# Four product tiles instead of three, the softmax subtraction and the statistics placed earlier, and one block of convolution products placed a slice later

## The chip, the cores and the metric

One core of one Trainium2 chip. The metric is device time in microseconds of the whole program, median of the runs; lower is better.

## The reference

The input is 16 images of 56 x 56 pixels with 384 channels, float32. Two layers, each added to its input:

```python
x = x + attention(group_norm(x), w_qkv, w_proj, b_proj)
x = x + depthwise_3x3(group_norm(x), sign(clip(w)))
```

- `group_norm`: 32 groups of 12 channels, over all pixels of an image.
- `attention`: a 1x1 projection to q, k, v. The 384 channels form three groups of 128, with dilations 1, 2, 3. In each group of four heads of 32 channels, every pixel attends to its 3 x 3 neighbours at that dilation: nine scores per head, softmax, weighted sum of v. Then a 1x1 output projection with bias.
- `depthwise_3x3`: each channel convolved with its own 3 x 3 kernel of signs, zero padding.

## The kernel before

**Tiling.** Channels lie on partitions, in three blocks of 128. An image is cut into 7 chunks of 8 rows, 448 pixels. Each chunk goes through three plans: `plan_a` (load, transpose, channel statistics of the input), `plan_b` (the attention layer, residual and statistics of its result, written to DRAM as `x1d`), `plan_c` (the convolution layer and the output). The 112 chunks are pipelined: while `plan_b` works on chunk m, `plan_a` is some chunks ahead and `plan_c` ten chunks behind.

**Order of the work.** Time is counted in slices, nine to a chunk (`STEP`). Each plan registers small pieces with `at(slice, order, piece)`; at the end the pieces are emitted sorted by slice, and inside a slice by the constants `SOFTMAX, SCORE, STATISTICS, CONVOLVE, WEIGH, ... PROJECT, ... LOADS`. A scheduler then takes this emitted program and decides on each engine's own instruction order, from its estimate of when each instruction is ready, with the emitted order as priority. Each engine runs its list in order. Tiles come from pools with a fixed number of buffers; a new tile takes the buffer that came free longest ago, and its writer waits until the last reader of that buffer is done.

**Attention of one chunk (`plan_b`).**
- `score(i)`, nine times: VectorE (DVE) writes `t` = q times three shifted k (L517), TensorE (PE) adds them over the head's channels into `ps` (L502).
- `softmax_1` to `softmax_5`: ScalarE (ACT) copies `ps` to `sT` (L534), PE transposes, DVE takes maximum and difference (L540, L541), ACT the exponential (L542), DVE the sum, reciprocal and product `ew` (L546 to L548). ACT casts `ew` to bf16 into `e3` (`e<-ew`, L556). GpSimd (POOL) computes `rest` = `ew` minus that cast (L560, `softmax_4`) and writes two further bf16 terms of it (L564, L565, `softmax_5`). The sum of the three terms stands for the float32 weight.
- `turn_weights`: a transposing DMA from SP's queue turns `e3` into `aT` (L570). It cannot start before L565 is done.
- `weigh(i)`, nine times, three for each group: PE spreads the weights over channels into the single PSUM tile `pb_a` (L583, three matmuls), DVE multiplies by v into a tile `w` (L590), and POOL adds the second and the third `w` of a group to the first (L598), then the three thirds to `y` (L601, L602). `w` has three buffers.
- `out_project`: PE (L616), DVE adds bias and residual into `xr` (L619) and takes statistics (L622).

**Convolution of one chunk (`plan_c`).** Channels 0 to 255 go through PE: `load` brings three shifted copies of `x1d` into `z` (L684), ACT normalises them (`z<-z`, L697, four instructions per block), POOL zeroes the padding before and after (L678, L699), PE convolves (L711), DVE adds (L718). Channels 256 to 383 go through ACT and POOL: ACT normalises into `zg` (L740), `taps_g(ky)` writes three products (`m<-zg`, L762), POOL adds the blocks (L768) and the thirds (L773, L776). In the first chunk of an image (`c == 0`) the whole group is one slice later (`late = 1`), since the statistics of that image are only just there. `turn(s)` transposes back through `osb` (L788), sent out from SP's queue (L791).

**Statistics.** `statistics(when, sets)` runs `group_norm` in six steps; the first aggregates per-channel statistics with six instructions (L310) at one slice. From the third image on, each call serves the second layer of image b and the first layer of image b + 2 at once.

**Last image.** `plan_c` of image 15 borrows tiles of the attention, `w` among them (`z_last`, L675).

Of the kernel before, what the change touches and what calls it, by code (L numbers as in the profile page):

```python
# [8 lines left out]
F32 = mybir.dt.float32  # L9
# [8 lines left out]
P = 128  # L18
HEADS = 4
HD = 32  # L20
NG = 3
# [3 lines left out]
SUB = 112  # L25
# [3 lines left out]
NPAD = 32  # L29
# [6 lines left out]
def dilated_attention_then_binary_conv(  # L36
# [28 lines left out]
    nc = tc.nc  # L65
    B, H, W, C = x.shape
    PX = ROWS * W
    NCH = H // ROWS
    NSUB = PX // SUB
# [12 lines left out]
    of = out.rearrange("b h w c -> b (h w) c")  # L82
# [65 lines left out]
    xn_p = ctx.enter_context(tc.tile_pool(name="xn_p", bufs=3))  # L148
    xr_p = ctx.enter_context(tc.tile_pool(name="xr_p", bufs=1))
    t_p = ctx.enter_context(tc.tile_pool(name="t_p", bufs=4))  # L150
    w_p = ctx.enter_context(tc.tile_pool(name="w_p", bufs=3))
    y_p = ctx.enter_context(tc.tile_pool(name="y_p", bufs=4))
    s_p = ctx.enter_context(tc.tile_pool(name="s_p", bufs=1))
    a_p = ctx.enter_context(tc.tile_pool(name="a_p", bufs=2))
    x1_p = ctx.enter_context(tc.tile_pool(name="x1_p", bufs=2))
    xg_p = ctx.enter_context(tc.tile_pool(name="xg_p", bufs=2))
    m_p = ctx.enter_context(tc.tile_pool(name="m_p", bufs=3))
    o_p = ctx.enter_context(tc.tile_pool(name="o_p", bufs=3))


    kv = []
# [134 lines left out]
    def group_norm(sets):  # L296

        had = {}
        L = len(sets)

        def channels():
            had["ch"] = ch = st_p.tile([P, L, NG, 2], F32, tag=f"ch{L}", name="ch")
            for n, (stats, _, _) in enumerate(sets):
                for j in range(NG):
                    nc.vector.bn_aggr(ch[:, n, j, :], stats[:, j].rearrange("p c s -> p (c s)"))  # L310

        def mean():
            had["pair"] = pair = st_p.tile([GN_G, L, 3], F32, tag=f"pair{L}", name="pair")
            pm = ps_mt.tile([P, 512], F32, tag="mt", name="pm")
            for j in range(NG):
                nc.tensor.matmul(
                    pm[:GN_G, 0:L], gsel[:, j], had["ch"][:, :, j, 0], start=(j == 0), stop=(j == NG - 1)
                )
            nc.vector.tensor_scalar_mul(pair[:, :, 2], pm[:GN_G, 0:L], -1.0 / GN_CH)

        def deviation():

            ch = had["ch"]
            pb = ps_mt.tile([P, 512], F32, tag="mt", name="pb")
            for j in range(NG):
                nc.tensor.matmul(
                    pb[:, j * L : (j + 1) * L], gselT[:, j], had["pair"][:, :, 2], start=True, stop=True
                )
            had["dev"] = dev = st_p.tile([P, L, NG], F32, tag=f"dev{L}", name="dev")
            nc.vector.tensor_tensor(  # L330
                dev, pb[:, : NG * L].rearrange("p (j l) -> p l j", l=L), ch[:, :, :, 0], ALU.add
            )
            nc.gpsimd.tensor_tensor(dev, dev, dev, ALU.mult)
            nc.gpsimd.tensor_tensor(dev, dev, ch[:, :, :, 1], ALU.add)

        def variance():
            dev = had["dev"]
            pv = ps_mt.tile([P, 512], F32, tag="mt", name="pv")
            for j in range(NG):
                nc.tensor.matmul(pv[:GN_G, 0:L], gsel[:, j], dev[:, :, j], start=(j == 0), stop=(j == NG - 1))  # L340
            had["var"] = var = st_p.tile([GN_G, 3, L], F32, tag=f"var{L}", name="var")
            v, r = var[:, 0], var[:, 1]
            nc.vector.tensor_scalar(v, pv[:GN_G, 0:L], 1.0 / GN_CH, 1e-5, op0=ALU.mult, op1=ALU.add)

            ri = r.bitcast(I32)
            nc.vector.tensor_single_scalar(ri, v.bitcast(I32), 1, op=ALU.arith_shift_right)
            nc.vector.tensor_scalar(ri, ri, -1, RSQRT_BITS, op0=ALU.mult, op1=ALU.add)

        def invert():

            var, pair = had["var"], had["pair"]
            v, r, t = var[:, 0], var[:, 1], var[:, 2]
            for step in range(3):
                nc.gpsimd.tensor_tensor(t, r, r, ALU.mult)
                nc.gpsimd.tensor_tensor(t, t, v, ALU.mult)
                nc.gpsimd.tensor_scalar(t, t, -0.5, 1.5, op0=ALU.mult, op1=ALU.add)
                nc.gpsimd.tensor_tensor(pair[:, :, 1] if step == 2 else r, r, t, ALU.mult)
            nc.gpsimd.tensor_tensor(pair[:, :, 0], pair[:, :, 2], pair[:, :, 1], ALU.mult)

        def spread_out():  # L360
            pair = had["pair"]
            pp = ps_mt.tile([P, 512], F32, tag="mt", name="pp")
            for j in range(NG):
                nc.tensor.matmul(
                    pp[:, 2 * L * j : 2 * L * (j + 1)], gselT[:, j], pair[:, :, 0:2], start=True, stop=True
                )
            mr = st_p.tile([P, NG, L, 2], F32, tag=f"mr{L}", name="mr", bufs=5 - L)
            nc.vector.tensor_copy(mr.rearrange("p j l s -> p (j l s)"), pp[:, : 2 * L * NG])
            for n, (_, done, for_convolution) in enumerate(sets):
                if not for_convolution:  # L370
                    done(mr[:, :, n])
                    continue

                pz = ps_mt.tile([P, 512], F32, tag="mt", name="pz")
                for s in range(JG * NQ):
                    of_set = gselT[:, s // NQ, s % NQ * HD : s % NQ * HD + HD]
                    for ky in range(3):
                        nc.tensor.matmul(
                            pz[ky * HD : (ky + 1) * HD, 2 * s : 2 * s + 2], of_set, pair[:, n, 0:2],
                            start=True, stop=True,  # L380
                        )
                mrz = st_p.tile([K3, JG, NQ, 2], F32, tag="mrz", name="mrz")
                nc.vector.tensor_copy(mrz.rearrange("p j q s -> p (j q s)"), pz[:K3, : 2 * JG * NQ])
                done(mr[:, :, n], mrz)

        return channels, mean, deviation, variance, invert, spread_out
# [6 lines left out]
    def at(when, order, piece):  # L393

        pieces.setdefault((when, order), []).append(piece)
# [50 lines left out]
    def plan_b(m, t0):  # L446
# [83 lines left out]

        def softmax_1():

            sT = s_p.tile([P, PX], F32, tag="sT", name="sT")
            nc.scalar.copy(sT, had.pop("ps")[:, :PX])  # L534
            pt = ps_mt.tile([P, 512], F32, tag="mt", name="pt_s")
            for s in range(NSUB):
                nc.tensor.transpose(pt[:SUB, s * P : (s + 1) * P], sT[:, s * SUB : (s + 1) * SUB], permf)
            pt4 = pt[:SUB].rearrange("p (s v) -> p s v", s=NSUB)[:, :, :NR]
            mx = s_p.tile([SUB, NSUB, GH], F32, tag="mx", name="mx")
            nc.vector.reduce_max(mx, by_neighbour(pt4).rearrange("p s o k -> p s k o"), axis=AX.X)  # L540
            nc.vector.tensor_tensor(by_neighbour(weights), by_neighbour(pt4), over_neighbours(mx), ALU.subtract)  # L541
            nc.scalar.activation(weights, weights, AF.Exp, scale=SCALE)  # L542
# [13 lines left out]
            nc.scalar.copy(term[0], e8)  # L556

        def softmax_4():
            had["rest"] = rest = s_p.tile([SUB, NSUB * NPAD * HEADS], F32, tag="rest", name="rest")
            nc.gpsimd.tensor_tensor(rest.rearrange(EIGHTS, k=8), e8, term[0], ALU.subtract)  # L560

        def softmax_5():
# [72 lines left out]
        at(t0 + 9, SOFTMAX, softmax_1)  # L635
        at(t0 + 10, SOFTMAX, softmax_2)
        at(t0 + 11, SOFTMAX, softmax_3)
        at(t0 + 11, PROJECT, softmax_4)
        at(t0 + 12, SOFTMAX, softmax_5)
        at(t0 + 12, LOADS, turn_weights)  # L640
        for i in range(9):
# [5 lines left out]
    def plan_c(m, t0):  # L647
# [110 lines left out]
        def taps_g(ky):  # L758
            t = m_p.tile([P, 3, PX], F32, tag="m", name="m")
            for kx in range(3):  # L760
                o = 3 * ky + kx
                nc.scalar.activation(  # L762
                    rows(t[:, kx]), zp[:, ky : ky + ROWS, kx : kx + W], AF.Copy, scale=ktap[:, o : o + 1]
                )
            if ky == 0:
                had["m"] = t
            else:
                nc.gpsimd.tensor_tensor(had["m"], had["m"], t, ALU.add)  # L768
# [39 lines left out]

        late = 1 if c == 0 else 0
        at(t0 - 4, LOADS, load_g)  # L810
        at(t0 - 1 + late, NORM, normalise_g)
        for ky in range(3):
            at(t0 + 2 * ky + late, CONVOLVE, lambda ky=ky: taps_g(ky))
        for kx in (1, 2, 3):
            at(t0 + 5 + kx, CONVOLVE, lambda kx=kx: sum_g(kx))
        at(t0 - 1, LOADS, load_x)
# [30 lines left out]
    def statistics(when, sets):  # L847

        steps = {}

        def norm(k):
            if k == 0:
                steps["of"] = group_norm([
                    (stats1.pop(b), lambda mr, mrz, b=b: mr1.update({b: (mr, mrz)}), True) if layer
                    else (stats0.pop(b), lambda mr, b=b: mr0.update({b: mr}), False)
                    for layer, b in sets
                ])
            steps["of"][k]()

        for k in range(6):  # L860
            at(when + STAT_SLICE[k], STAT_ORDER[k], lambda k=k: norm(k))

    for b in range(2):
# [39 lines left out]
```

## Time and profile before

| | |
|---|---|
| median of 3 runs | 5359.44 us (5357.7 to 5360.04) |
| the profiled execution: its own time | 5363.24 us |
| its span, first to last instruction | 5361.5 us |
| PE busy | 5146.8 us, 96% |
| POOL busy | 4254.0 us, 79% |
| DVE busy | 4173.9 us, 78% |
| ACT busy | 2310.0 us, 43% |
| granted TensorE clock | 0.978 |

The busy time of PE is that of its matmuls, with modelled ends; what matters below is the time in which its list stood still, and for whom. In the trace's timeline a line gives start, duration, engine, source line, operation and tiles, and in brackets the idle time of that engine just before it with whoever ended it. In a list of waits the columns are total, number of times and longest wait.

### The profile page before, as it was taken

Reading aid. Unit: us, or ns where it says so; the run is one execution under the profiler, and the core shown is the slowest. Engines: PE = TensorE matmul, PEld = TensorE weight load, DVE = VectorE, ACT = ScalarE, POOL = GpSimd, SP = SyncE. Lnnn points to the kernel's source line nnn. Section 1 sums busy time; section 2 is a strip of 40 time slices with the busy share of each in tenths; the row PEclk is TensorE's granted clock in tenths of the full one; section 3 lists DMA queues with packets and bytes.
Section 4 is the critical chain, followed back from the end, with each engine's and each line's share of the span. In section 5 each row is a group of like instructions: output and inputs, shape, how many; then the busy total and the mean of one; then the engine's idle time right before and its main releaser. Section 6 shows DMA issues by size and latency. Waiting matters only on the chain. (4 is left out here: it accounts for less than half of the span.)

```text
span 5361.5 us, 75511 instructions
## 1 busy us (share of the span) xinstructions
PE 5146.8 (96%) x26885; PEld 2339.3 (44%) x26885; DVE 4173.9 (78%) x4125; ACT 2310.0 (43%) x4077; POOL 4254.0 (79%) x2950
## 2 busy tenths in 40 slices
PE   8999999999999999999999999999999999999976
PEld 4444444444444444444444444444444444444433
DVE  5887887778778777887878877777887878877764
ACT  3213444444444444444444444444434444444434
POOL 2777888888888887878888888888888888788881
PEclk8999999999999999999999999999999999999986
DMA  6434555555555555555555555565555555544455
GB/s 192 135 108 113 166 161 162 161 155 162 155 164 157 152 159 162 166 155 161 161 154 166 147 161 161 160 165 154 165 158 155 162 147 164 146 135 134 130 135 154
DMA packets 811631, 825.62 MB, mean 154 GB/s; under 512 B 360307, under 2 KB 801014, under 8 KB 811254
## 3 DMA queue, kind: packets, MB, share of 16 engines
q1 hardware_dynamic: 803270, 808.79, 54.7%
q10 hardware_dynamic: 7984, 12.00, 0.7%
q8 instruction: 213, 3.49, 0.3%
q14 instruction: 164, 1.34, 0.1%
HBM read 466.41 MB, written 231.21 MB: 130 GB/s over the span
## 5 line engine op out<-in xcount | busy, mean ns | idle before, releaser
L598 POOL TENSOR_TENSOR w<-w 128x1344 f32<-128x1344 f32 x672 | 2069.9, 3080 | 587.3 <-DVE w L590 544.6
L590 DVE TENSOR_TENSOR w<-pb_a,v 128x1344 f32<-128x1344 f32 x1008 | 1555.7, 1543 | 327.4 <-PE pb_a L583 213.9
L517 DVE TENSOR_TENSOR t<-pq,k 128x1344 f32<-128x1344 f32 x1008 | 1536.2, 1551 | 252.0 <-PE pq L464 251.6
L464 PE MATMUL pkv<-xn,wqkvT 128*128 128x448 f32 x3924 | 1567.6, 548 | 0.4 <-DVE xr L619 0.4
L464 PEld LDWEIGHTS pkv<-xn,wqkvT 128*128 128x128 f32 x3924 | 718.0, 190 | 670.7 <-issue 644.9
L464 PE MATMUL pq<-xn,wqkvT 128*128 128x448 f32 x1962 | 858.8, 573 | 0.0
L616 PE MATMUL po<-y,wprojT 128*128 128x448 f32 x2016 | 832.8, 549 | 23.9 <-POOL y L602 18.4
L697 ACT ACTIVATE z<-z,mrz 96x448 f32<-96x448 f32 x840 | 578.2, 751 | 631.6 <-DMA z<-x1d 371.5
L768 POOL TENSOR_TENSOR m<-m 128x1344 f32<-128x1344 f32 x210 | 640.1, 3048 | 147.4 <-ACT m L762 143.1
L502 PE MATMUL ps<-t,sel 128*32 128x448 f32 x6048 | 663.5, 548 | 45.0 <-DVE t L517 44.3
L762 ACT ACTIVATE m<-zg,ktap 128x448 f32<-128x448 f32 x945 | 555.5, 659 | 8.6 <-POOL xg L776 1.7
L616 PEld LDWEIGHTS po<-y,wprojT 128*128 128x128 f32 x2016 | 375.6, 191 | 381.5 <-issue 339.5
L711 PE MATMUL pc<-z,kdiag 96*32 96x440 f32 (+1 forms) x5040 | 517.5, 544 | 6.1 <-POOL z L699 4.4
L464 PEld LDWEIGHTS pq<-xn,wqkvT 128*128 128x128 f32 x1962 | 353.0, 194 | 330.3 <-issue 330.3
L583 PE MATMUL pb_a<-aT,spread 24*128 24x448 bf16 x3024 | 369.9, 360 | 82.6 <-DMA aT<-e 60.6
L602 POOL TENSOR_TENSOR y<-y,w 128x448 f32<-128x448 f32 x336 | 381.2, 1134 | 16.4
L601 POOL TENSOR_TENSOR y<-w 128x448 f32<-128x448 f32 x336 | 381.3, 1135 | 13.7
L619 DVE SCALAR_TENSOR_TENSOR xr<-po,bias,xr 128x448 f32<-128x448 f32 x336 | 227.9, 678 | 208.5 <-PE po L616 203.8
L474 ACT COPY v<-pkv 128x448 f32<-128x448 f32 x336 | 176.3, 525 | 493.7 <-PE pkv L464 484.7
L718 DVE TENSOR_TENSOR x<-pc,x 128x448 f32<-128x448 f32 x224 | 139.0, 621 | 310.4 <-PE pc L711 309.3
L583 PEld LDWEIGHTS <-spread 24*128 24x128 bf16 x3024 | 100.3, 91 | 571.1 <-issue 488.5
L474 ACT COPY k<-pkv 128x448 f32<-128x448 f32 x336 | 178.9, 532 | 377.2 <-PE pkv L464 377.2
(132 smaller groups left out, 4278.3 us busy)
## 6 DMA issues: line engine op xcount, KB each, us to landing
z<-x1d SPq DMA_DIRECT2D x570, 224.0 KB, 3.8
xr<-xd SPq DMA_DIRECT2D x112, 672.0 KB, 4.2
x1d<-xr SPq DMA_DIRECT2D x112, 672.0 KB, 3.2
xn<-xd SPq DMA_DIRECT2D x109, 672.0 KB, 4.6
xin<-in_x_dram SPq DMA_DIRECT2D x105, 672.0 KB, 7.2
xd<-xa SPq DMA_DIRECT2D x315, 224.0 KB, 3.3
out_dram<-osb SPq DMA_DIRECT2D x420, 168.0 KB, 3.5
x<-x1d SPq DMA_DIRECT2D x112, 448.0 KB, 8.1
```

The source lines that it names most:

```text
L464: nc.tensor.matmul(dst[:, :PX], wqkvT[:, cc, o0 : o0 + P], had["xn"][:, cc, :], start=(cc == 0), stop=(cc == NG - 1))
L502: return nc.tensor.matmul(had["ps"][32 * j : 32 * j + 32, :PX], sel[:, s0 : s0 + 32], tk, start=(issued[j] == 1), stop=(issued[j] == len(r ...
L517: nc.vector.tensor_tensor(t.rearrange("p k (r w) -> p k r w", w=W), q3, k3, ALU.mult)
L583: return nc.tensor.matmul(pb[:, kx, :PX].rearrange("p (s n) -> p s n", s=NSUB), spread[rows_of, v % 2, :], had["a"][rows_of, :, v // 8, :] ...
L590: nc.vector.tensor_tensor(w.rearrange("p k (r w) -> p k r w", w=W), pb[:, :, :PX].rearrange("p k (r w) -> p k r w", w=W), three(kv[1][g][m ...
L598: nc.gpsimd.tensor_tensor(w0, w0, w, ALU.add)
L601: nc.gpsimd.tensor_tensor(y, w0[:, 0], w0[:, 1], ALU.add)
L616: nc.tensor.matmul(po[:, :PX], wprojT[:, g, j * P : (j + 1) * P], had[f"y{g}"], start=(g == 0), stop=(g == NG - 1))
L697: nc.scalar.activation(z, z, AF.Identity, bias=mrz[:, j, q, 0:1], scale=mrz[:, j, q, 1:2])
L711: return nc.tensor.matmul(pcr[q * HD : (q + 1) * HD, :, lo:hi], kdiag[:, kx, j * NQ + q, :], rows(set_of(j, q))[:, :, lo + kx - 1 : hi + k ...
L762: nc.scalar.activation(rows(t[:, kx]), zp[:, ky : ky + ROWS, kx : kx + W], AF.Copy, scale=ktap[:, o : o + 1])
L768: nc.gpsimd.tensor_tensor(had["m"], had["m"], t, ALU.add)
```

## The change

- The pool of `w` has four buffers instead of three.
- The pool of `osb` has two instead of three.
- `rest` no longer has a buffer of its own: it shares the one buffer of `sT`, which is made large enough for both.
- `softmax_4`, the subtraction on POOL, is registered with order `SOFTMAX` instead of `PROJECT` in the same slice, so it is emitted ahead of everything else there.
- The aggregations of the first-layer set are registered one channel block at a time, three, two and one slices ahead of the others. The others stay at their slice.
- In an image's first chunk, `normalise_g` and the three `taps_g` are two slices late instead of one; the normalisation and convolution of `z`, and the sums, stay.

```diff
-    w_p = ctx.enter_context(tc.tile_pool(name="w_p", bufs=3))
+    w_p = ctx.enter_context(tc.tile_pool(name="w_p", bufs=4))
...
-    o_p = ctx.enter_context(tc.tile_pool(name="o_p", bufs=3))
+    o_p = ctx.enter_context(tc.tile_pool(name="o_p", bufs=2))
...
-        def channels():
-            had["ch"] = ch = st_p.tile([P, L, NG, 2], F32, tag=f"ch{L}", name="ch")
-            for n, (stats, _, _) in enumerate(sets):
-                for j in range(NG):
-                    nc.vector.bn_aggr(ch[:, n, j, :], stats[:, j].rearrange("p c s -> p (c s)"))
+        def channels(n, j):
+            if "ch" not in had:
+                had["ch"] = st_p.tile([P, L, NG, 2], F32, tag=f"ch{L}", name="ch")
+            nc.vector.bn_aggr(had["ch"][:, n, j, :], sets[n][0][:, j].rearrange("p c s -> p (c s)"))
...
-            sT = s_p.tile([P, PX], F32, tag="sT", name="sT")
+            sT = s_p.tile([P, NSUB * NPAD * HEADS], F32, tag="sT", name="sT")[:, :PX]
...
-            had["rest"] = rest = s_p.tile([SUB, NSUB * NPAD * HEADS], F32, tag="rest", name="rest")
+            had["rest"] = rest = s_p.tile([P, NSUB * NPAD * HEADS], F32, tag="sT", name="rest")[:SUB]
...
-        at(t0 + 11, PROJECT, softmax_4)
+        at(t0 + 11, SOFTMAX, softmax_4)
...
         late = 1 if c == 0 else 0
         at(t0 - 4, LOADS, load_g)
-        at(t0 - 1 + late, NORM, normalise_g)
+        at(t0 - 1 + 2 * late, NORM, normalise_g)
         for ky in range(3):
-            at(t0 + 2 * ky + late, CONVOLVE, lambda ky=ky: taps_g(ky))
+            at(t0 + 2 * ky + 2 * late, CONVOLVE, lambda ky=ky: taps_g(ky))
...
-        def norm(k):
-            if k == 0:
+        def norm(k, *which):
+            if not steps:
                 steps["of"] = group_norm([
-                    (stats1.pop(b), lambda mr, mrz, b=b: mr1.update({b: (mr, mrz)}), True) if layer
-                    else (stats0.pop(b), lambda mr, b=b: mr0.update({b: mr}), False)
+                    (stats1[b], lambda mr, mrz, b=b: mr1.update({b: (mr, mrz)}), True) if layer
+                    else (stats0[b], lambda mr, b=b: mr0.update({b: mr}), False)
                     for layer, b in sets
                 ])
-            steps["of"][k]()
+            steps["of"][k](*which)
 
-        for k in range(6):
+        for n, (layer, _) in enumerate(sets):
+            for j in range(NG):
+
+                sooner = 3 - j if n and not layer else 0
+                at(when - sooner, STATISTICS, lambda n=n, j=j: norm(0, n, j))
+        for k in range(1, 6):
             at(when + STAT_SLICE[k], STAT_ORDER[k], lambda k=k: norm(k))
```

## The prediction

> **What bounds the kernel now.** I read the engine totals first: PE is busy 96% of the span, so a change pays only where PE stands still. Next PE's waits in the steady stretch from 560 to 4640 us, where three kinds of stall are nearly everything:
>
> ```profile
> PE pb_a L583 <- DMA aT<-e: 47.1, 12, 4.0
> PE ps L502 <- DVE t L517: 33.5, 28, 1.5
> PE pb_a L583 <- DVE w L590: 3.9, 12, 0.4
> ```
>
> The aT stall comes once per image and the other two about twice. Then DVE's waits in the same stretch, for what makes `t` and `w` late:
>
> ```profile
> DVE w L590 <- POOL w L598: 41.8, 30, 1.9
> DVE w L590 <- POOL e L564: 10.9, 12, 0.9
> ```
>
> So `w` waits for a buffer that POOL still reads. The timelines of PE, DVE and POOL around 2318 us show one case from end to end:
>
> ```profile
> 2319.85 0.37 PE L583 MATMUL pb_a<-aT,spread 24*128 24x448 bf16 x3 [0.34 <-DVE w L590]
> 2322.14 1.71 PE L502 MATMUL ps<-t,sel 128*32 128x448 f32 x16 [1.46 <-DVE t L517]
> ...
> 2318.24 1.56 DVE L590 TENSOR_TENSOR w<-pb_a,v 128x1344 f32<-128x1344 f32 x1 [1.93 <-POOL w L598]
> 2319.71 0.91 DVE L546 TENSOR_REDUCE sm<-ew 112x48 f32<-112x432 f32 x1
> 2320.54 1.55 DVE L517 TENSOR_TENSOR t<-pq,k 128x1344 f32<-128x1344 f32 x1
> ...
> 2315.17 3.03 POOL L598 TENSOR_TENSOR w<-w 128x1344 f32<-128x1344 f32 x1
> ```
>
> DVE stood 1.93 us until POOL's addition ended at 2318.20; the `t` queued behind that `w` came late, and PE lost 0.34 + 1.46 = 1.80 us. Last, the same timelines at an image's first convolution chunk:
>
> ```profile
> 2407.07 3.05 POOL L768 TENSOR_TENSOR m<-m 128x1344 f32<-128x1344 f32 x1 [2.31 <-ACT m L762]
> 2410.06 0.27 POOL L699 MEMSET z<- 32x224 f32 x1
> 2412.51 3.06 POOL L598 TENSOR_TENSOR w<-w 128x1344 f32<-128x1344 f32 x1 [2.18 <-DVE w L590]
> ...
> 2425.22 1.15 POOL L560 TENSOR_TENSOR rest<-ew,e 112x512 f32<-112x512 f32 x1
> ...
> 2434.32 0.55 PE L583 MATMUL pb_a<-aT,spread 24*128 24x448 bf16 x3 [3.91 <-DMA aT<-e]
> 2434.80 4.85 PE L464 MATMUL pq<-xn,wqkvT 128*128 128x448 f32 x6
> ```
>
> POOL runs without a pause from 2412.51 to `rest` at 2425.22 and on to L565 (ends 2430.24); SP issues the transpose at 2430.28, it lands about 4.0 us later, PE goes on at 2434.32.
>
> **What the Trainium skill says.** "Perfetto Trace Analysis", section "Tensor Engine Instruction (MATMUL, LD_WEIGHTS)": ACT, DVE and GpSimd are strict first-in first-out. The trace agrees: `t` at 2320.54 needed nothing from POOL. "TensorE: Matmul & The Clock Gate", section "Part 1: The HAM clock gate": about 3.4 us without work put TensorE at half rate. The trace agrees: the six `pq` matmuls take 4.85 us after the 3.91 us stall, 2.52 elsewhere, while `ps` keeps its 1.71 after 1.46 us. Over the twelve stalls the six take 54.5 us instead of 12 x 2.52 = 30.2, so 24 us come on top of 47.1. "SBUF — State Buffer", section "SBUF: two separate sides": a DVE operation with two SBUF inputs and a GpSimd operation lock each other out. The trace agrees: L548, both inputs in SBUF, takes 0.59 us in a gap of POOL (2324.30) and 2.12 us at 2416.94, ending 0.5 us after POOL's addition. L590 reads PSUM and keeps its 1.5 us.
>
> **The change, part by part.** I compared the two built programs engine by engine. PE, with all 19,567 matmuls and loads, has the same order. So has DVE, aggregations included, except three operations near the end. In POOL the subtraction keeps its place. **Subtraction first and spread aggregations therefore cost and bring nothing**: the scheduler had already put them there by readiness. What is left:
>
> *Fourth w.* Each `w` now waits for what the `w` before it waited for: the second `w` of a group no longer needs the third of the group before freed. At 2318 us that `w` can start at 2316.3, when DVE is free; its buffer came free at 2308.5 (end of the addition begun 2305.48). `w` ends 2317.8, the sum 2318.6, `t` 2320.1. PE wants it at 2322.14 - 1.80 = 2320.34: no stall. The whole 33.5 + 3.9 = 37.4 us of the stretch is of this kind (every one of these stalls has a buffer wait of DVE before it, and 41.8 less two idle waits of 0.5 covers the sum). What is late next: L548 comes 1.9 us earlier and meets POOL's addition of 2320.61 to 2323.66, so it ends about 2324.2, still before the old 2324.9; the `x` and `w` behind it are at most 0.2 us late, and the next `t` has 0.6 us of waiting to spare. The chunk's aT lands at about 2336.8 for a `pb_a` at 2339.5, so 1.8 us earlier still fits. In the last two images before 5125 us four such stalls lose 0.56, 0.17, 0.43 and 0.34, together 1.5. At 467 to 496 us PE waits 4.5 us for `w`; the last two, 3.2 us, go, but the first output projection then meets POOL's `y` at about 500: I take 2. After 5156 us POOL is nearly continuous up to the last `y` and holds PE; its own gaps waiting for `w` are 2.0, 0.7 and 1.1: I take 2 of at most 3.8. Sum: 37.4 + 1.5 + 2 + 2 = 42.9 us gained.
>
> *Products later.* Per image one thing moves. ACT's list was `zg`, four `z`, `sT`, three products, three products, four `z`, three `xn`; now the second three products come after the second four `z`. No DMA moves in the steady part; five SP issues swap places in the last image only. ACT's total is unchanged (products 0.58 each, `z` 0.68 each), so `xn` still starts at 2409.5; nothing behind it, `v` and `k` copies included, is later. The second `z` block is now wanted at 2405.25, 1.6 us sooner; its last load was issued at 2395.58 and loads of `z` land after 3.8 us, so it is there by 2400. On POOL the memset L699 changes places with the first addition L768, which waits for the second products: 2403.51 + 1.74 + 2.71 + 1.74 = 2409.65, end 2412.7 instead of 2410.1. POOL's 2.18 us wait for `w` hides most of it: the L598 behind it starts at 2412.73 instead of 2412.51, and from there to aT nothing is idle. So **the aT stall grows by 0.22 us**, twelve times 2.6 us; bounds 0 (it can't shrink, the chain is busy) and 0.7 with some more half-rate time.
>
> *osb.* With two buffers a copy waits for the output two before. Tightest: copies at 2414.34 and 2420.38; the first is issued at 2415.25 and outputs land in 2.1 to 5.3 us, so before 2420.6. Should it be late, ACT has 4.5 us idle after the next copy. I take 0; bounds 0 and 0.2 us a chunk, 20 us.
>
> *rest in sT.* `rest` waits for the transposes of `sT`, `sT` for L565 of the chunk before; at 2403 us that is over 20 us past. 0, with nothing else to bound.
>
> *Sum:* 42.9 - 2.6 = 40.3 us off the profiled 5363.2, 5323; this execution lies 3.8 us above the median of the runs, so 5359.4 - 40.3 = **5319 us**.
>
> **Rivals.** (1) *Half comes back.* POOL, 79% busy, takes the gain elsewhere, by L548's lock or a later `y` or aT. For: the lock is in the trace. Against: PE's next need has 0.2 to 2.7 us to spare. Half of 37.4 is 18.7: 5338. (2) *The aT stall goes too*, as the change's words suggest, by POOL reaching `rest` sooner. Against: its order, and a chain without a gap. It would be 47.1 + 24 more and no 2.6: 5246. (3) *Slower.* The moved products stand behind `z` in ACT's queue; if that block's loads come late, products, L768, `rest` and aT slip one for one. From 42.9 / 12 = 3.6 us a time this decides. With 5 us, such waits as ACT has for `z` in other chunks (longest 6.0), it costs 60 or more: about 5377. Against: loads in place 5 us before. (4) *No change*: DVE starts `w` sooner, but PE's waits stay, since POOL, not the buffer, sets DVE's pace. About 5357. Against: POOL has idle time before each chunk's next additions.
>
> **How the numbers follow.** My forecast 0.72, (1) 0.15, (2) 0.04, (3) 0.04, (4) 0.05. A measurement here can tell 0.2%, 10.7 us, from no change. Faster: the first three, 0.91; same 0.05; slower 0.04. The range runs from 5300 (the start and the tail at their bounds, 3 us more, and a fifth of the 71 us of the aT stall gone instead of 2.6 added) to 5345 (osb at its bound, 20 us, and the aT stall at its, 6 us more; or half lost), leaving out (2) to (4).
>
> **What would show it.** Right: DVE's `w` waits for POOL all but gone in the stretch; `ps` for `t` and `pb_a` for `w` under 4 us there; aT still twelve stalls of about 4.1 us with slow `pq` behind; `rest` on POOL in the same place; chunk periods unchanged elsewhere. Wrong: stalls of `ps` near 1 us remaining, aT stalls gone or over 5 us, or ACT waiting at `osb`.

## The result, and the profile after

Median 5321.69 us (5317.59 to 5330.1, 4 runs) against 5359.74 us for the kernel before (5357.7 to 5362.44, 4 runs): ratio 0.9931, 95% interval 0.9914 to 0.9948. The forecast was 5319. The profiled execution of the changed kernel has a span of 5319.5 us (before 5361.5), PE busy 5131.9 us, DVE 4206.4, POOL 4255.7. All source lines named below have moved up by one: L590 is now L589, L598 L597, L502 L501, L768 L767, `rest` L559, and so on.

PE's waits in the steady stretch, now 560 to 4620 us (total, number, longest). The list is complete:

```profile
PE pb_a L582 <- DMA aT<-e: 49.3, 12, 4.4
PE po L615 <- ACT v L473: 8.9, 15, 1.1
```

The stalls of `ps` for `t` and of `pb_a` for `w`, 37.4 us together before, are not small: they are absent. The aT stall is there twelve times as before, 2.2 us more in all. A third one grew, `po` for ACT, from 3.1 us in 7 times. DVE's waits for POOL in the same stretch:

```profile
DVE w L589 <- POOL e L563: 8.9, 12, 0.8
DVE w L589 <- POOL m L767: 7.1, 5, 1.4
```

`w <- POOL w`, 41.8 us before, has gone from the list. The twelve waits for `e` lie at aT's chunk, as before; the five for `m` lie elsewhere, and PE waits for none of them. One more wait for POOL, of 0.8 us, is left out here.

The case that the prediction followed from end to end, in the changed kernel's timelines of PE and DVE, the same chunk some 17.6 us sooner:

```profile
2304.56 1.71 PE L501 MATMUL ps<-t,sel 128*32 128x448 f32 x16
...
2300.58 1.55 DVE L589 TENSOR_TENSOR w<-pb_a,v 128x1344 f32<-128x1344 f32 x1
2302.04 0.91 DVE L545 TENSOR_REDUCE sm<-ew 112x48 f32<-112x432 f32 x1
2302.86 1.55 DVE L516 TENSOR_TENSOR t<-pq,k 128x1344 f32<-128x1344 f32 x1
```

No bracket of idle time stands behind `w`, nor behind `ps`: DVE goes from the operation before into `w`, the sum and `t`, and `t` ends 0.15 us before PE takes it up.

Now the first convolution chunk of an image in the timelines of POOL and PE:

```profile
2392.12 3.06 POOL L767 TENSOR_TENSOR m<-m 128x1344 f32<-128x1344 f32 x1 [1.43 <-ACT m L761]
2395.14 3.05 POOL L597 TENSOR_TENSOR w<-w 128x1344 f32<-128x1344 f32 x1
2398.16 3.02 POOL L767 TENSOR_TENSOR m<-m 128x1344 f32<-128x1344 f32 x1
...
2407.82 1.18 POOL L559 TENSOR_TENSOR rest<-ew,e 112x512 f32<-112x512 f32 x1
2408.94 1.16 POOL L601 TENSOR_TENSOR y<-y,w 128x448 f32<-128x448 f32 x1
2410.02 0.63 POOL L563 CAST e<-rest 112x512 bf16<-112x512 f32 x1
2410.59 1.18 POOL L775 TENSOR_TENSOR xg<-m,xg 128x448 f32<-128x448 f32 x1
2411.70 1.20 POOL L564 TENSOR_TENSOR e<-rest,e 112x512 bf16<-112x512 f32 x1
...
2416.97 0.36 PE L582 MATMUL pb_a<-aT,spread 24*128 24x448 bf16 x3 [4.12 <-DMA aT<-e]
2417.26 4.14 PE L463 MATMUL pq<-xn,wqkvT 128*128 128x448 f32 x6
```

But for a memset, the order is that of before. `sT` on ACT lies at 2385.52, at 2403.08 before: 17.56 us apart. On the old scale the addition of `w` behind the first products starts at 2395.14 + 17.56 = 2412.70 (predicted 2412.73, 2412.51 before) and L564 ends at 2412.90 + 17.56 = 2430.46 (2430.24 before); the stall is 4.12 us instead of 3.91. The six `pq` behind it run slowly again.

Where the 42.0 us between the two profiled spans lie, cut at the same `pb_a` (that of 398.51, 814.26, 4379.33 and 5016.02 us before, found again at 397.83, 808.00, 4343.04 and 4971.70), with the prediction's own terms put into the same stretches (rounded, so that the column misses its sum by 0.1):

| stretch of before | before, us | after, us | measured | predicted |
|---|---|---|---|---|
| to 398.5 | 398.5 | 397.8 | -0.7 | 0 |
| to 814.3 | 415.8 | 410.2 | -5.6 | -4.4 |
| to 4379.3 (eleven images) | 3565.1 | 3535.0 | -30.0 | -29.0 |
| to 5016.0 | 636.7 | 628.7 | -8.0 | -4.5 |
| to the end | 345.5 | 347.8 | +2.3 | -2.3 |
| sum | | | -42.0 | -40.3 |

In the eleven images that is 324.1 us an image before and 321.4 after; the runs below are compared by this period too.

### The profile page after: what moved, and what is told of

It reads as the page before. It is cut to its first block, busy times and chain, and to the rows that moved or that the text cites. A ratio compares the mean times of both kernels' runs of the same rounds, so it can differ in the third digit from the quotient of the medians.

```text
span 5319.5 us, 75544 instructions
## 1 busy us (share of the span) xinstructions
PE 5131.9 (96%) x26885; PEld 2336.3 (44%) x26885; DVE 4206.4 (79%) x4125; ACT 2311.5 (43%) x4077; POOL 4255.7 (80%) x2950
## 5 line engine op out<-in xcount | busy, mean ns | idle before, releaser
L597 POOL TENSOR_TENSOR w<-w 128x1344 f32<-128x1344 f32 x672 | 2071.6, 3083 | 497.6 <-DVE w L589 474.9
L589 DVE TENSOR_TENSOR w<-pb_a,v 128x1344 f32<-128x1344 f32 x1008 | 1555.1, 1543 | 277.4 <-PE pb_a L582 235.4
L767 POOL TENSOR_TENSOR m<-m 128x1344 f32<-128x1344 f32 x210 | 640.0, 3047 | 133.7 <-ACT m L761 129.5
L501 PE MATMUL ps<-t,sel 128*32 128x448 f32 x6048 | 659.7, 545 | 7.9 <-DVE t L516 7.1
```

What stands on the lines that cost most here:

```text
L501: return nc.tensor.matmul(had["ps"][32 * j : 32 * j + 32, :PX], sel[:, s0 : s0 + 32], tk, start=(issued[j] == 1), stop=(issued[j] == len(r ...
L589: nc.vector.tensor_tensor(w.rearrange("p k (r w) -> p k r w", w=W), pb[:, :, :PX].rearrange("p k (r w) -> p k r w", w=W), three(kv[1][g][m ...
L597: nc.gpsimd.tensor_tensor(w0, w0, w, ALU.add)
```

## The experiments

Every ratio below is to the kernel before on the same chip.

**1. Three tiles of w again.** On each engine the instructions stand exactly in the changed kernel's order.

```diff
-    w_p = ctx.enter_context(tc.tile_pool(name="w_p", bufs=4))
+    w_p = ctx.enter_context(tc.tile_pool(name="w_p", bufs=3))
```

> The changed kernel with three tiles of w again, all else of the change kept; on every engine the instructions stand in the changed kernel's order. Theory (the fourth tile brings all of the gain): in the steady stretch DVE's w waits about 42 us for POOL's w again, ps for t about 33 us and pb_a for w about 4; the time is that of the kernel before plus the 2.6 us of the moved products, about 5362 us (5355 to 5368). Rival (part of the gain comes from another part of the change): those stalls come back only in part and the time lies well below 5350.

Measured 5363.37 us, ratio 1.0011 (1.0003 to 1.0019). PE's and DVE's waits from 560 to 4640 us:

```profile
PE pb_a L582 <- DMA aT<-e: 49.2, 12, 4.2
PE ps L501 <- DVE t L516: 28.8, 24, 1.5
PE pb_a L582 <- DVE w L589: 3.4, 10, 0.4
...
DVE w L589 <- POOL w L597: 38.3, 30, 1.9
```

The old stalls are back, with the changed kernel's aT stall beside them; the period is 324.3 us, 0.2 above that of before. The fourth tile is thus worth 0.9931 / 1.0011 = 0.992, some 43 us (33 to 53 by the two intervals), and all else of the change costs 0.1% or so. The tiles of `osb` and the buffer of `rest` that the change gives up belong to it all the same: a `w` takes 5.25 KB of a partition (1344 float32 values), and these two give back 1.5 and 1.75.

**2. The products back.**

```diff
-        at(t0 - 1 + 2 * late, NORM, normalise_g)
+        at(t0 - 1 + late, NORM, normalise_g)
...
-            at(t0 + 2 * ky + 2 * late, CONVOLVE, lambda ky=ky: taps_g(ky))
+            at(t0 + 2 * ky + late, CONVOLVE, lambda ky=ky: taps_g(ky))
```

> The changed kernel with the products of an image's first chunk (and the normalisation of its last group of channels) where they were before. Theory (the moved products delay the second addition on POOL, and with it rest and aT, by 0.2 us an image): the twelve aT stalls go from 4.1 back to 3.9 us each, the time is about 2.6 us below the changed kernel, 5319 us. Rival (the move brought part of the gain): aT stalls stay at 4.1 or grow, the time rises to 5330 or more.

Measured 5320.18 us, ratio 0.9928 (0.9916 to 0.9941). The aT stalls are 47.4 us instead of 49.3, 3.92 to 3.96 each but for one of 4.19; the period is 320.9 us, 0.5 less. In total this can't be told from the changed kernel; the stalls and the period go the way of the theory. Without the moved products, the regrouped statistics and the earlier subtraction leave every engine's list as the three buffer edits alone make it: their zero holds by the order of the instructions.

**3. Two tiles of osb in the kernel before.**

```diff
-    o_p = ctx.enter_context(tc.tile_pool(name="o_p", bufs=3))
+    o_p = ctx.enter_context(tc.tile_pool(name="o_p", bufs=2))
```

> The kernel before with two tiles of osb in place of three and nothing else. Up to the last image all engines keep their order; there, in POOL's list, both additions of products go ahead of the last addition of w, as they do in the changed kernel. Theory as predicted: nothing, 5359 us, no wait of ACT for an output's store. Theory now: the last y on POOL comes about 5 us later, and the kernel ends 2 to 5 us later, 5361 to 5364 us; no other stretch differs. Rival (osb's bound): ACT waits for stores in every chunk, 20 us more, 5380.

Measured 5359.77 us, ratio 1.0007 (0.9999 to 1.0015): the bound of 20 us is excluded. The 3.7 us by the ratio fit the newer expectation and zero alike. Its twelve aT stalls lie at 3.9 us as before, and its period is 323.9 us, 0.2 less than before. The last output projection starts 37.4 us after the one at 5203.31 us (5240.73), in the kernel before 33.3 (5203.17 to 5236.45): the last `y` is 4.1 us late. In this execution it is more than made up behind it: the end comes 118.1 us after that projection's start instead of 125.0.

**4. rest ahead of y.** In the one chunk of each image that meets the first convolution chunk:

```diff
+        def ahead():
+            return tc.high_priority() if m % NCH == 2 and m > NCH else nullcontext()
...
-            nc.gpsimd.tensor_tensor(rest.rearrange(EIGHTS, k=8), e8, term[0], ALU.subtract)
+            with ahead():
+                nc.gpsimd.tensor_tensor(rest.rearrange(EIGHTS, k=8), e8, term[0], ALU.subtract)
...
-            nc.gpsimd.tensor_copy(term[1], r8)
-            nc.gpsimd.tensor_tensor(term[2], r8, term[1], ALU.subtract)
+            with ahead():
+                nc.gpsimd.tensor_copy(term[1], r8)
+                nc.gpsimd.tensor_tensor(term[2], r8, term[1], ALU.subtract)
```

> The changed kernel with the subtraction that makes rest, and the two operations behind it, given priority in the one chunk of each image that meets an image's first convolution chunk: on POOL rest goes ahead of the first y operation and the last step ahead of the addition to xg. Nothing is left out. Theory (aT waits for a chain of POOL without a gap, so what is taken out of it comes off the stall): aT is issued 2.3 us sooner, twelve stalls fall from 4.1 to about 1.9 us, the six pq matmuls behind each return from 4.4 to about 2.5 us, two stalls of 1.9 go; about 26 + 23 + 4 = 53 us, 5269 us. Rival (POOL is the bound there, so the time moves to w and y): stalls shrink, PE waits for w, t or y instead, at least half comes back: 5295 or more.

Measured 5306.77 us, ratio 0.9902 (0.9887 to 0.9917), some 15 us below the changed kernel, not 53. The timelines of POOL and PE:

```profile
2402.60 1.16 POOL L563 TENSOR_TENSOR rest<-ew,e 112x512 f32<-112x512 f32 x1
2403.71 1.14 POOL L605 TENSOR_TENSOR y<-w 128x448 f32<-128x448 f32 x1
2404.79 0.62 POOL L568 CAST e<-rest 112x512 bf16<-112x512 f32 x1
2405.36 1.14 POOL L606 TENSOR_TENSOR y<-y,w 128x448 f32<-128x448 f32 x1
2406.45 1.17 POOL L569 TENSOR_TENSOR e<-rest,e 112x512 bf16<-112x512 f32 x1
2407.58 1.15 POOL L780 TENSOR_TENSOR xg<-m,xg 128x448 f32<-128x448 f32 x1
...
2411.72 0.56 PE L587 MATMUL pb_a<-aT,spread 24*128 24x448 bf16 x3 [3.03 <-DMA aT<-e]
2412.20 4.85 PE L463 MATMUL pq<-xn,wqkvT 128*128 128x448 f32 x6
```

My expectation mis-sized the step: `rest` has changed places with one `y`, but both `y` still stand ahead of the last step L569; only the addition to `xg`, 1.1 us, has left the chain. The stall fell by just that, from 4.1 to 3.0 us (35.9 us in all), and no new wait of PE for `w`, `t` or `y` came. The time lies where the rival had it, but not for the rival's reason. The chain theory holds one for one; the size of the step was wrong, and the slow `pq` stayed in ten of twelve cases.

**5 and 6. rest on DVE, and the same with the products back.**

```diff
+        def aside():
+            return nc.vector if m % NCH == 2 and m > NCH else nc.gpsimd
...
-            nc.gpsimd.tensor_tensor(rest.rearrange(EIGHTS, k=8), e8, term[0], ALU.subtract)
+            aside().tensor_tensor(rest.rearrange(EIGHTS, k=8), e8, term[0], ALU.subtract)
...
-            nc.gpsimd.tensor_copy(term[1], r8)
-            nc.gpsimd.tensor_tensor(term[2], r8, term[1], ALU.subtract)
+            aside().tensor_copy(term[1], r8)
+            aside().tensor_tensor(term[2], r8, term[1], ALU.subtract)
```

> The changed kernel with rest and the two operations behind it on DVE in place of POOL, in the one chunk of each image that meets an image's first convolution chunk. Nothing is left out. Theory (aT waits for POOL's list and nothing else): DVE can take rest when the e cast of ACT ends, POOL's list no longer holds it, aT is issued about 5 us sooner and lands before PE asks: the twelve stalls of 4.1 us and the half-rate pq behind them (about 23 us over all) are gone; against it DVE has three more operations an image, some 2 us, of which PE sees between nothing and 22 us in all. Time 5245 to 5270, most likely 5255. Rival (DVE is then late: t and w wait for the cast of ACT, since DVE's list is in order): PE's ps and pb_a stalls appear in these chunks at 1 to 2 us each, 5280 or more.

> As the run with rest on DVE, and the products of an image's first chunk where they were before the change. Theory (the moved products only lengthen POOL's chain to aT, and aT no longer hangs on it): no difference from the run with rest on DVE, within 3 us. Rival (the products also hold up w or y on POOL): 5 us or more between the two.

Measured 5302.68 us, ratio 0.9889 (0.9873 to 0.9905), and 5297.71 us, ratio 0.9881 (0.9864 to 0.9897). PE's waits of the first of them from 560 to 4600 us, the list complete:

```profile
PE ps L501 <- DVE t L516: 24.4, 12, 2.0
PE po L618 <- ACT v L473: 10.6, 17, 1.1
PE pb_a L585 <- DVE w L592: 8.6, 12, 0.8
```

and its timelines of DVE and PE at the same place:

```profile
2393.46 0.82 DVE L562 TENSOR_TENSOR rest<-ew,e 112x512 f32<-112x512 f32 x1 [0.73 <-ACT e L555]
2394.20 1.54 DVE L592 TENSOR_TENSOR w<-pb_a,v 128x1344 f32<-128x1344 f32 x1
2395.67 1.81 DVE L566 CAST e<-rest 112x512 bf16<-112x512 f32 x1
...
2402.17 0.37 PE L585 MATMUL pb_a<-aT,spread 24*128 24x448 bf16 x3 [0.71 <-DVE w L592]
...
2405.10 2.54 PE L501 MATMUL ps<-t,sel 128*32 128x448 f32 x16 [2.03 <-DVE t L516]
```

The aT stall is gone, as the theory said: it came from POOL's list. But the rival's stalls are there. DVE's list grew not by 2 us but by 0.73 + 0.82 + 1.81 + 0.71 = 4.07 us (the last subtraction is 0.71), and PE loses 0.7 + 2.0 us of the 4.1 gained. Nor did PE get back all that the slow `pq` had cost: behind the stalls of 2.0 us `ps` now ran slowly in seven of the twelve cases (2.0 to 3.2 us instead of 1.71), and PE's busy time in the eleven images fell by 10.2 us, 0.9 an image, where the slow `pq` had cost 1.9. The period is 319.2 us, only 2.2 below the changed kernel's. My 5255 fell here.

**7 and 8. The cast on ACT, and the same with the products back.**

```diff
+        meets = m % NCH == 2 and m > NCH
...
+            eng = nc.vector if meets else nc.gpsimd
+            eng.tensor_tensor(rest.rearrange(EIGHTS, k=8), e8, term[0], ALU.subtract)
...
+            if meets:
+                nc.scalar.copy(term[1], r8)
+                nc.vector.tensor_tensor(term[2], r8, term[1], ALU.subtract)
```

> As the run with rest on DVE, but the cast between its two subtractions is on ACT, which is idle there; DVE keeps the two subtractions. Nothing is left out. Theory (what eats the gain of the run with rest on DVE is the 4.1 us by which DVE's list grew: 0.73 waiting, 0.82, 1.81 for the cast, 0.71): DVE's list grows by 2.3 us, so PE's stalls of 0.7 for w and 2.0 for t in these chunks fall to under 1 us together; some 1.8 us twelve times, 22 us, are gained on that run: about 5281 us, aT still without a stall. Rival (the stalls come from rest standing ahead of w in the list, not from the sum, or ACT's later xa copy holds PE): PE still loses 2 us or more a chunk, 5295 or more.

> As the run with the cast on ACT, and the products of an image's first chunk where they were before the change. Theory (with aT off POOL's chain the place of the products matters to nothing): within 3 us of the run with the cast on ACT. Rival (the products' place still costs some us elsewhere, as the 5 us between the two runs with rest on DVE hint): 3 to 8 us less.

Measured 5281.32 us, ratio 0.9857 (0.984 to 0.9873), and 5278.33 us, ratio 0.9852 (0.9837 to 0.9866). The number is the one expected, but by luck: the mechanism holds only in part. DVE and PE in the first of them:

```profile
2385.15 0.81 DVE L562 TENSOR_TENSOR rest<-ew,e 112x512 f32<-112x512 f32 x1 [0.73 <-ACT e L555]
2385.89 1.55 DVE L596 TENSOR_TENSOR w<-pb_a,v 128x1344 f32<-128x1344 f32 x1
2387.36 2.08 DVE L568 TENSOR_TENSOR e<-rest,e 112x512 bf16<-112x512 f32 x1
...
2393.48 0.43 PE L789 MATMUL pt_o<-ident,x 128*112 128x128 f32 x2 [0.66 <-DVE x L724]
...
2394.94 0.37 PE L589 MATMUL pb_a<-aT,spread 24*128 24x448 bf16 x3 [0.92 <-DVE w L596]
...
2396.40 2.97 PE L501 MATMUL ps<-t,sel 128*32 128x448 f32 x16 [0.57 <-DVE t L516]
```

The last subtraction, 0.71 us in run 5, now meets an addition of POOL and takes 2.08, so DVE's list still grew by 3.6 us. PE loses 0.9 us for `w`, 0.6 for `t` and 0.7 for `pt_o` (the transposes of the output) in such a chunk, over 2 us as the rival said, and `ps` behind them ran slowly in seven of the twelve (2.6 to 3.2 us instead of 1.71). The period is 318.7 us, 0.6 below run 5: over the eleven images 6 of the 20 us between the two profiled spans. Of the rest, 4 us lie ahead of 791 us, 2 in the two images behind the eleven, 7 in the tail; why those parts were shorter is open. Both kernels beat the changed one and the one before.

The three pairs with and without the moved products (2 and the changed kernel, 6 and 5, 8 and 7) differ by 1.6, 4.3 and 2.7 us by their ratios, all to the side that the products cost time, none outside its intervals. Run 8 lies within its 3 us; between the theory of run 6 (within 3 us) and its rival (5 or more) the runs do not decide.

## Why the prediction was right

**The fourth w: right, mechanism and size.** The stretch's 37.4 us went as worked out, `w` started when DVE was free, and the run with three tiles undoes it. (The stall of `pb_a` for `w` came once per image, 12 times, not about twice as the prediction says of both; the sum is not touched.) What the prediction named as late next is there: the product `ew` comes sooner and meets POOL's addition more often. The two groups of DVE over the eleven images, before and after:

```profile
L548 DVE TENSOR_TENSOR ew<-ew,sm 112x432 f32<-112x432 f32 x77 | 62.6, 813 | 0.0
```

```profile
L547 DVE TENSOR_TENSOR ew<-ew,sm 112x432 f32<-112x432 f32 x77 | 91.9, 1194 | 0.0
```

29 us more of DVE, as the Trainium skill ("SBUF — State Buffer", section "SBUF: two separate sides") says of operations that lock each other out; none of it reached PE, as the slack promised, so rival (1) had its cost and not its effect. Over the whole program `ew` takes 38.8 us more (92.0 to 130.8), which is more than the 32.5 by which DVE's busy time rose while the kernel got faster.

**A gain that the prediction missed.** It read from one case that `ps` keeps its 1.71 us behind a stall of 1.46. Behind three of the 28 stalls of the stretch `ps` did run slowly; the first of them, in the kernel before:

```profile
2692.28 3.21 PE L502 MATMUL ps<-t,sel 128*32 128x448 f32 x16 [1.17 <-DVE t L517]
```

The others took 2.98 us (at 3988.95) and 3.21 us (at 4637.91). In the changed kernel's stretch there is none, in run 1 there are five: they come and go with the stalls.

**A wait that the prediction missed:** `po` for ACT's `v`, from 3.1 to 8.9 us. It comes with the fourth tile: 2.9 us in run 1, 7.9 in run 2. PE now arrives sooner at a PSUM tile that ACT has yet to empty; at 2010.87 us, for one, ACT was in seven products (2006.36 to 2010.39) with the `v` copy queued behind them. The prediction looked for what is late next on DVE and POOL, not on ACT. It did not show in the sum because PE's own busy time fell by 5.8 us in the eleven images (3487.8 to 3482.0), 2.8 of them in the two slow `ps` that lie there; what shortened the rest isn't settled.

**The moved products: right.** Predicted 0.22 us a time and 2.6 in all; the stalls grew by 2.2, and the paired runs point the same way, by 1.6 to 4.3, none of them clear of noise. ACT's second block of `z` did not wait for its loads (2387.65 us, straight behind the products), so the rival that ends slower had no ground.

**The scheduler edits: right at zero,** aT's stall stayed, and rival (2) with it was refuted: emitting the subtraction sooner did not move it in POOL's list.

**osb and the tail: an effect was missed.** The prediction took 2 us of gain after 5156 us, and priced two tiles of `osb` as a wait of ACT, 0. In the steady stretch that is right. But the pool's size changes the scheduler's order in the last image. POOL before, then after:

```profile
5228.11 3.02 POOL L598 TENSOR_TENSOR w<-w 128x1344 f32<-128x1344 f32 x1 [1.08 <-DVE w L590]
5231.09 3.01 POOL L768 TENSOR_TENSOR m<-m 128x1344 f32<-128x1344 f32 x1
5234.06 1.13 POOL L601 TENSOR_TENSOR y<-w 128x448 f32<-128x448 f32 x1
```

```profile
5184.19 6.12 POOL L767 TENSOR_TENSOR m<-m 128x1344 f32<-128x1344 f32 x2
5190.26 3.01 POOL L597 TENSOR_TENSOR w<-w 128x1344 f32<-128x1344 f32 x1
5193.23 1.13 POOL L772 TENSOR_TENSOR m<-m 128x448 f32<-128x448 f32 x1
```

Two additions of products, 6.1 us, stand ahead of the last `w`, and PE's last wait for `y` is 11.36 us, 7.70 before; that projection starts 38.5 us after the one at 5159.18 us, where it was 33.3. Run 3 shows the same swap from `osb` alone. The prediction had seen that lists differ near the end, though it does not name POOL's, and gave it no price.

The whole tail came out 4.6 us above the prediction's term (+2.3 for -2.3). That this is the swap's cost is not shown: run 3, with the swap, has a tail of 342.9 us, and run 2, with the swap and four tiles of `w`, one of 343.4, both below the 345.5 of before. In single executions the tail scatters by more than the term.

The two stretches of the start gave 1.9 us more than predicted (6.3 for 4.4), the one behind the eleven images 3.5 more (8.0 for 4.5). These cover the tail, so that the sum lies nearer than its parts: that much is luck. The 30.0 for 29.0 of the eleven images hide such a pair too, the 5.8 us that `po` cost more (2.0 to 7.8 there) and the 5.8 by which PE's busy time fell; the 31.4 us of stalls for `t` and `w` that went there are no luck.

## What to carry to other kernels

When a wait for a buffer stands in an engine's in-order list, price it by the other engine's next need behind it, and then ask each engine in turn, those off the critical path too, who is late once the list moves up. Compare the built order of the instructions before pricing an edit of priorities or of a pool's size: here two edits moved nothing and one small pool reordered the end. A chain that ends in a transfer is shortened only by what really leaves it; moving work to a second busy engine gives much of the gain back through that engine's own list.

## What was not expected of the hardware

- TensorE ran slowly after much shorter stalls than the prediction's 3.4 us (the Trainium skill, "TensorE: Matmul & The Clock Gate", section "Part 1: The HAM clock gate", which calls the window free-running). After the stalls of 3.9 to 4.4 us of the two kernels the six `pq` were slow each time; after stalls of 2.95 to 3.05 us, in run 4, they took 3.7 to 4.85 us in ten of twelve cases and 2.52 in two; after one stall of 1.94 us in the changed kernel four `pq` took 3.34 instead of 1.77. `ps` was slow behind three of the 28 stalls before (each 1.17 or 1.18 us), behind seven of twelve of 2.0 us in run 5, and behind seven of twelve of only 0.57 us in run 7, where two other short stalls stand just ahead. A shorter stall mostly made a slow start less sure, but no length between 0.6 and 4.1 us was a sharp limit, and the idle time of one stall alone doesn't tell. The page's idle window of about 3.4 us is no lower limit for a stall here.
- A cast on DVE with a single input in SBUF seems to be held as well: f32 to bf16, 112 x 512, begun at 2395.67 us in run 5, took 1.81 us and ended 0.28 us after POOL's addition (2393.69 to 2397.20), as the products `ew` do. No cast of that run stood clear of POOL, so its own time is not shown; the shortest took 1.25. That addition of POOL, which had met `rest` on DVE at its start, took 3.51 us instead of 3.06.
